# A graph-network kernel: rows of the third pair gathered into unused memory of the sums, six destination loads moved from ScalarE's queue to SyncE's, and x's loads ordered by SyncE's program

## The chip, the core and the metric

The kernel runs on one core of one Trainium2 chip. The metric is the device time in microseconds (us), the median of repeated runs. The engines are named as in the profile: PE (TensorE, with its weight loads as PEld), DVE (VectorE), ACT (ScalarE), POOL (GpSimd) and SP (SyncE, which here only issues transfers). A "q" after an engine's name (SPq, ACTq) marks work of its instruction queue, such as issuing a DMA.

## The reference

One layer of message passing over N = 6250 nodes of 128 features and 100,000 edges, sorted by destination:

```python
msg_in = concat([x[src], x[dst]])            # 100000 x 256
h = relu(msg_in @ Wm1 + bm1)                 # 256 -> 256
h = relu(h @ Wm2 + bm2)                      # 256 -> 256
messages = h @ Wm3 + bm3                     # 256 -> 128
agg = segment_sum(messages, dst) / clip(count(dst), 1)
upd = relu(concat([x, agg]) @ Wn1 + bn1) @ Wn2 + bn2
out = layernorm(x + (x + upd))
```

All inputs are float32, the indices int32.

## The kernel before, in words

The work has three stages.

**Preparation, blocks 0 to 12.** Nodes are taken in 13 blocks of 4 x 128. PE turns a block of x (`turn`, L307) and multiplies it by the two halves of `Wm1` (`products`, L258). The products with the first half, the A table, go through ACT (L266) to device memory (`atab`, stores L267 on SP). The products with the second half, the B table, are split by ACT, DVE and POOL into three bf16 terms, written into seven slots of 768 columns of the third plane of `acc` (`acc[:, HC, ...]`, which is not yet needed for the sums), and stored to `btab` (L276 on SP). The B table runs five blocks behind the A table. ACT, POOL, PE and SP follow the program's order here; DVE is placed by the scheduler. Each load or store on SP also waits, in the built program, until the transfer eight places before it among those of SP and ACT has landed.

x comes in loads of two blocks (`load_x`, L172 on SP). Four of them are held back by a one-column DVE copy that reads the turned block `behind` (L171), so that they are not issued before it. The table `X_LOADS = {0: (4, 6), 1: (6, 8), 3: (8, 10), 5: (10, 12)}` says at the top of which block which load stands. The weights `wu1`, `w3` and `w2` are held back in the same way to block 6 (L189, L191 to L193). In blocks 10 to 12 ACT issues the destinations of the first three pairs of groups (`destinations`, L384: two loads a pair, each broadcast to 64 partitions), held back by a DVE copy from `srcT` (L380).

At the end of preparation PE, ACT and DVE also make the part of the node update that needs x alone (`x_part`, L355, L358, L360), a block at a time, and a small matmul for the bias `b23` (`pb3`, L451, and DVE L452).

**Edges, 98 pairs of groups of 512.** In turn `i` of the loop, `fetch` has POOL gather the A rows of pair `i` with eight indirect DMAs (L492, 128 rows of 1 KB each) and SP load eight windows of B rows (L498; for pair 0 ACT loads four of them). Both go into one of two buffers, `rows`, so the gather of pair `i` waits until the first layer of pair `i - 2` has read its buffer. In the same turn, with `p = i - 1`, the order on PE is: `turned` of pair `p - 3` (L584), `first_layer` of pair `p` (32 transposes L533, then 16 products with a one-hot matrix L540), `sums` of pair `p - 2` (L565), `second_layer` of pair `p - 1` (32 matmuls L555). ACT makes `h1` (L546) and copies the sums (L573); DVE makes the one-hot matrices (`make_hot`, L516, L519), takes the second layer's results (L557) and adds the sums to `acc` (L594).

Before the first sums are added, the seven slots of `acc` are cleared on DVE (`clear`, L644): three in turn `p = 0` ahead of the first layer, two in each of `p = 1` and `p = 2`. One block of `x_part`, number `X_FIRST = 9`, is made in turn `p = 0` behind the first layer, its two results taken by ACT (L358) and DVE (L360).

**Nodes.** The sums are divided, updated, normalised and stored.

## Time and profile before

| | before |
|---|---|
| median of 6 runs | 1707.39 us (1701.44 to 1725.05) |
| the profiled execution | 1709.8 us |
| its span, first to last instruction | 1708.0 us |
| PE busy | 1335.6 us, 78% of the span |
| POOL busy | 811.2 us, 47% |
| granted PE clock over the span | 0.859 of full speed |
| indirect gathers, L492 | 784, 946 ns each at the median |

By stage, from a table of windows of the same execution:

| window, us | what runs | PE busy | granted clock | DMA share |
|---|---|---|---|---|
| 0 to 81.6 | preparation, to pair 0's first transpose | 75.90 | 0.98 | 0.84 |
| 81.6 to 142.8 | pairs 0 to 3 enter the pipeline | 41.06 | 0.81 | 0.42 |
| 142.8 to 1600 | the edge loop | 1119.08 | 0.85 | 0.39 |
| 1600 to 1708 | last pairs and the nodes | 99.59 | 0.97 | 0.32 |

A row of the timeline reads: start and length in us, engine, line of the kernel, operation, what is written from what, how many instructions were merged, and in brackets the idle time before it with what ended that idle time. "issue" means that the engine waited for nothing that the profile shows, "remote" that nothing recorded fits as the releaser. The DMA share is the mean busy share of the core's 16 DMA engines.

### The profile page before, as it was taken

What the parts mean: (1) busy time and instruction counts of PE and PEld (TensorE: products, weight loads), DVE (VectorE), ACT (ScalarE), POOL (GpSimd) and SP (SyncE); (2) the same over time, 40 slices, a digit from 0 to 9 for tenths busy, and PEclk for the clock granted to TensorE, in tenths of its full rate; (3) what the DMA queues carried; (4) which work ended last, traced back from release to release, by engine and by line L of the source; (5) the groups of instructions that cost most, each with busy time, mean ns of one, the idle gap of its engine ahead of it and who ended that gap; (6) DMA issues with size and microseconds to landing.
All of it is one profiled execution on the core that took longest, in us unless ns stands there. A gap on an engine that the chain in (4) does not pass through costs nothing. (4 is left out here: it accounts for less than half of the span.)

```text
span 1708.0 us, 32156 instructions
## 1 busy us (share of the span) xinstructions
PE 1335.6 (78%) x11222; PEld 1054.5 (62%) x11223; DVE 657.0 (38%) x2073; ACT 379.6 (22%) x768; POOL 811.2 (47%) x871
## 2 busy tenths in 40 slices
PE   9868778767777877877877877877788777778898
PEld 8556556656665655656655655665566566666656
DVE  6623323433433333332332332333333333333477
ACT  6412112212221221211211211221122212212136
POOL 8655445445444544445444445544555445445121
PEclk9978888888888888888888888888888888888899
DMA  8744344434434434424434433333443334333143
GB/s 312 260 113 119 94 108 119 114 90 121 114 93 120 117 94 112 114 86 123 113 91 115 108 85 112 106 95 98 112 112 104 92 103 109 93 96 106 40 113 110
DMA packets 167754, 193.69 MB, mean 113 GB/s; under 512 B 31074, under 2 KB 133428, under 8 KB 167572
## 3 DMA queue, kind: packets, MB, share of 16 engines
q0 software_dynamic: 38160, 103.75, 22.5%
q1 hardware_dynamic: 100640, 61.84, 12.3%
q10 hardware_dynamic: 28788, 26.01, 5.4%
q8 instruction: 89, 1.46, 0.4%
q14 instruction: 77, 0.63, 0.1%
HBM read 168.97 MB, written 22.88 MB: 112 GB/s over the span
## 5 line engine op out<-in xcount | busy, mean ns | idle before, releaser
L492 POOL DMA_INDIRECT rows<-atab,srcT x784 | 747.6, 954 | 795.7 <-PE ph L540 560.8
L555 PE MATMUL bank<-w,h 128*128 128x256 f32 x3128 | 710.0, 386 | 0.1
L555 PEld LDWEIGHTS bank<-w,h 128*128 128x128 f32 x3128 | 593.5, 192 | 132.9 <-PE bank L565 54.9
L557 DVE TENSOR_TENSOR h<-bank,nb 128x512 f32<-128x512 f32 x391 | 254.8, 688 | 965.9 <-remote 521.2
L546 ACT ACTIVATE h<-ph,b 128x512 f32<-128x512 f32 x392 | 236.7, 686 | 1239.6 <-PE ph L540 1226.4
L584 PE MATMUL bank<-ident,part 64*128 64x64 f32 x1173 | 103.5, 290 | 335.8 <-DVE h L557 317.3
L584 PEld LDWEIGHTS bank<-ident,part 64*128 64x128 f32 x1173 | 73.6, 184 | 382.6 <-DVE h L557 335.9
L533 PE MATMUL ph<-ident,rows 64*128 64x64 f32 x3128 | 190.3, 299 | 15.4 <-issue 14.2
L533 PEld LDWEIGHTS ph<-ident,rows 64*128 64x128 f32 x3128 | 177.9, 208 | 20.0 <-issue 17.2
L594 DVE TENSOR_TENSOR acc<-acc,bank 128x63 f32 x782 | 171.6, 219 | 33.4 <-DVE acc L594 2.1
L565 PE MATMUL bank<-h,oh 128*32 128x257 f32 x1564 | 150.6, 520 | 0.6 <-ACT part L573 0.6
L540 PE MATMUL ph<-oht,rows 64*128 64x128 bf16 x1564 | 108.6, 300 | 8.4 <-issue 6.4
L540 PEld LDWEIGHTS <-rows 64*128 64x128 bf16 x1564 | 92.9, 142 | 9.3 <-issue 7.2
L516 DVE TENSOR_SCALAR oht<-db,pbase 128x128 bf16<-128x128 int32 x392 | 95.0, 287 | 0.3
L565 PEld LDWEIGHTS bank<-h,oh 128*32 128x32 f32 x1564 | 51.6, 140 | 54.3 <-issue 28.0
L573 ACT COPY part<-bank 128x257 f32<-128x257 f32 x196 | 66.2, 399 | 22.1 <-PE bank L565 14.4
L519 DVE TENSOR_TENSOR oh<-iota_n,dloc 128x128 f32<-128x128 f32 x196 | 55.5, 283 | 0.0
L785 POOL TENSOR_TENSOR agg<-total,rc 128x512 f32<-128x512 f32 (+2 forms) x15 | 16.0, 1076 | 80.0 <-DMA x<-x2tab 41.1
L258 PE MATMUL pbt<-w,xT 128*128 128x256 f32 x196 | 46.4, 383 | 0.2 <-DVE rest L285 0.2
L258 PEld LDWEIGHTS pbt<-w,xT 128*128 128x128 f32 x196 | 36.3, 192 | 6.7 <-issue 1.7
L822 PEld LDWEIGHTS pot<-wu,u 128*128 128x128 f32 x192 | 23.6, 192 | 4.8 <-issue 4.3
L795 PE MATMUL put<-agg,wu 128*128 128x512 f32 (+2 forms) x60 | 23.9, 518 | 0.8 <-POOL agg L785 0.4
(134 smaller groups left out, 420.2 us busy)
## 6 DMA issues: line engine op xcount, KB each, us to landing
rows<-btab SPq DMA_DIRECT2D x778, 32.0 KB
db<-in_dst_dram ACTq DMA_DIRECT2D x194, 128.0 KB
rows<-atab,srcT POOLq DMA_INDIRECT x784
btab<-acc SPq DMA_DIRECT2D x24, 384.0 KB
atab<-at SPq DMA_DIRECT2D x24, 256.0 KB
xd<-in_x_dram SPq DMA_DIRECT2D x12, 256.0 KB
x2tab<-xd SPq DMA_DIRECT2D x12, 256.0 KB
x_sb<-in_x_dram SPq DMA_DIRECT2D x5, 512.0 KB
```

The costliest lines, as they stand in the source:

```text
L258: nc.tensor.matmul(pbt[:, a, :], xT[:, (t0 + a) * P:(t0 + a + 1) * P], w1[:, k, :], start=True, stop=True)
L492: nc.gpsimd.indirect_dma_start(out=ag[:, j, :], out_offset=None, in_=atab[:, :], in_offset=bass.IndirectOffsetOnAxis(ap=idx[:, j:j + 1], a ...
L516: nc.vector.tensor_scalar(ohts[:n, i, k, :], db[:n, k * P:(k + 1) * P], pb_cols[:n, k:k + 1], None, op0=ALU.is_equal)
L533: nc.tensor.matmul(ph[:, i, h, c, u * NQ:(u + 1) * NQ], ag[halves[h], u, c * P:(c + 1) * P], ident[halves[h], halves[h]], is_transpose=Tru ...
L540: nc.tensor.matmul(ph[:, i, h, c, k * P:(k + 1) * P], bw[halves[h], k, c * P:(c + 1) * P], ohts[halves[h], i, k, :], start=False, stop=Tru ...
L546: nc.scalar.activation(h1[:, i, c, :nh * 2 * P].rearrange("p (h e) -> p h e", h=nh), ph[:, i, :nh, c, :], AF.Relu, bias=b1[:, c:c + 1])
L555: nc.tensor.matmul(ph2[:, j - j0, :], h1[:, c, j * P:(j + 1) * P], w2[:, c, :], start=(c == 0), stop=(c == HC - 1))
L557: nc.vector.tensor_tensor(h2[:, j0:j0 + 2, :H], ph2, nb2.to_broadcast([P, 2, H]), op=ALU.max)
L565: nc.tensor.matmul(pg[j * WN:(j + 1) * WN, :H + 1], oh[:, j, :], h2[:, j, :], start=True, stop=True, skip_group_check=True)
L573: nc.scalar.copy(part[:nt * WN, i], pg[:nt * WN, :H + 1])
L584: nc.tensor.matmul(pts[h][:, i, c, :], rows, ident[halves[h], halves[h]], is_transpose=True, start=True, stop=True, skip_group_check=True)
L594: nc.vector.tensor_add(window, window, pts[h][:, i, :, k:k + WB])
```

## The change

Six things are changed together.

1. `fetch` takes the memory for its rows as an argument. For pair 2 (groups 4 and 5) it is `free_rows`, 2560 columns of the third plane of `acc` from slot 3 on. All other pairs keep the two `rows` buffers, which now go to pairs 0, 1, 3, 4, 5 and so on.
2. The slots are cleared in another order: slots 0 to 2 in turn `p = 0` and slots 3 to 6 in turn `p = 2`, both behind the first layer.
3. `x_part(X_FIRST)` is made inside the first layer of pair 0, between the transposes and the one-hot products, with DVE taking both results.
4. The destinations of pairs 0, 1 and 2 are issued by SP in blocks 0, 1 and 2 instead of by ACT in blocks 10, 11 and 12.
5. x's loads stand behind the A stores of their block on SP and lose their DVE copies; `w2` is loaded on SP in block 3 instead of block 6, without a copy.
6. The small matmul for `b23` stands ahead of the third of the last six blocks of `x_part` instead of behind them.

```diff
-            def load_x(b0, b1, behind=None):
+            def load_x(b0, b1):
                 t0, t1 = 4 * b0, 4 * b1
-                if behind is not None:
-                    nc.vector.tensor_copy(x_sb[:, t0, :1], xT[:, behind * 4 * P:behind * 4 * P + 1])
                 nc.sync.dma_start(x_sb[:, t0:t1, :].rearrange("p (b i) d -> p b i d", i=4), xb[:, b0:b1])
...
         def weights(block):
-            for t in (wu1, w3, w2):
+            for t in (wu1, w3):
...
-            nc.sync.dma_start(w2, wm2.rearrange("(k p) h -> p k h", p=P))
...
-        def destinations(g, ng, dst_row):
+        def destinations(g, ng, dst_row, queue=nc.scalar):
             db = ld.tile([P, 2, 2 * P], I32, name="db", bufs=3)
-            if isinstance(g, int) and g < 6:
-                nc.vector.tensor_copy(db[:, 0, :1], srcT[:, 0, :1])
...
-                nc.scalar.dma_start(db[h * NQ:(h + 1) * NQ, :ng, :], edges.to_broadcast([NQ, ng, 2 * P]))
+                queue.dma_start(db[h * NQ:(h + 1) * NQ, :ng, :], edges.to_broadcast([NQ, ng, 2 * P]))
...
         for i in range(BLOCKS):
-            if i in X_LOADS:
-                load_x(*X_LOADS[i], behind=i)
-                if X_LOADS[i][1] == BLOCKS - 1:
-                    nc.sync.dma_start(x_sb[:N - NTF * P, NTF, :], x[NTF * P:, :])
             for n, t0 in enumerate(range(4 * i, min(4 * i + 4, NT), 2)):
...
                 a_table(t0)
+            if i in X_LOADS:
+                load_x(*X_LOADS[i])
+                if X_LOADS[i][1] == BLOCKS - 1:
+                    nc.sync.dma_start(x_sb[:N - NTF * P, NTF, :], x[NTF * P:, :])
+            if i < 3:
+                early.append(destinations(2 * i, 2, dst_row, nc.sync))
+            if i == 3:
+                nc.sync.dma_start(w2, wm2.rearrange("(k p) h -> p k h", p=P))
             b_stores()
...
-            if BLOCKS - 3 <= i:
-                early.append(destinations(2 * len(early), 2, dst_row))
...
         for n, b in enumerate(behind):
+            if n == 2:
+                pb3 = pp.tile([P, 1], F32, name="pb3", tag="pp")
+                for c in range(HC):
+                    nc.tensor.matmul(pb3, w3[:, c, :], b2[:, c:c + 1], start=(c == 0), stop=(c == HC - 1))
+                nc.vector.tensor_add(b23, b3, pb3)
             whole(x_part(b, bank_pb, (nc.vector if n >= len(behind) - 2 else nc.scalar, nc.vector)))
...
-        def fetch(groups, queues):
+        ROWS = (GT + 1) * H
+        FREE = 3
+        free_rows = acc[:, HC, FREE * SLOT:FREE * SLOT + 2 * ROWS].rearrange("p (g r) -> p g r", g=2)
+        assert FREE * SLOT + 2 * ROWS <= SLOTS * SLOT
+        def fetch(groups, queues, rows=None):
-            rows = ld.tile([P, 2, (GT + 1) * H], F32, name="rows", bufs=2)
+            if rows is None:
+                rows = ld.tile([P, 2, ROWS], F32, name="rows", bufs=2)
...
-        def first_layer(got, ohts, nts):
+        def first_layer(got, ohts, nts, between=()):
...
+            whole(between)
...
-        slots = list(range(SLOTS))
+        slots = list(range(SLOTS))[::-1]
...
-                got = fetch([(srcT[:, 2 * i + k, :], firsts[k]) for k in range(2)], [q for q, _ in queues])
+                got = fetch([(srcT[:, 2 * i + k, :], firsts[k]) for k in range(2)], [q for q, _ in queues],
+                            free_rows if i == 2 else None)
...
-            if p == 0:
-                clear(3)
             if p < NP:
                 s = st[p]
-                s["h1"] = first_layer(s.pop("got"), s.pop("ohts"), s["nts"])
-            if p == 0:
-                whole(x_part(X_FIRST, bank, (nc.scalar, nc.vector)))
+                between = x_part(X_FIRST, bank, (nc.vector, nc.vector)) if p == 0 else ()
+                s["h1"] = first_layer(s.pop("got"), s.pop("ohts"), s["nts"], between)
+            if p in (0, 2):
+                clear(FREE if p == 0 else SLOTS - FREE)
...
-            if p in (1, 2):
-                clear(2)
```

More of the change, by code (lines that the diff above doesn't have):

```diff
@@ L447 @@
         for n, b in enumerate(behind):
+            if n == 2:
[3 more added lines that the diff above has]
+                nc.vector.tensor_add(b23, b3, pb3)
             whole(x_part(b, bank_pb, (nc.vector if n >= len(behind) - 2 else nc.scalar, nc.vector)))
-        pb3 = pp.tile([P, 1], F32, name="pb3", tag="pp")
-        for c in range(HC):
-            nc.tensor.matmul(pb3, w3[:, c, :], b2[:, c:c + 1], start=(c == 0), stop=(c == HC - 1))
-        nc.vector.tensor_add(b23, b3, pb3)
     late = ctx.enter_context(tc.tile_pool(name="late", bufs=1))
```

## The prediction

> **What bounds the kernel now.** I read the stages by windows first, then the timelines of POOL and PE over the stretch that the change touches, then the loop behind it.
>
> In preparation PE and the DMA engines are both full:
>
> ```profile
> 8.00:20.00 12.00, 12.00 (x67) 10.60 (x66) 8.32 (x14) 9.20 (x18) 11.63 (x17) 1.00 0.93 325
> 20.00:43.00 23.00, 23.00 (x121) 19.89 (x120) 14.59 (x31) 16.87 (x30) 19.64 (x25) 1.00 0.98 347
> 43.00:56.00 13.00, 12.83 (x57) 9.53 (x56) 9.63 (x13) 8.20 (x16) 11.40 (x14) 1.00 0.97 356
> ```
>
> PE is busy for 12.00 of 12 us, 23.00 of 23 and 12.83 of 13. The last three figures are the granted clock, the DMA share and GB/s. So a transfer moved inside these 48 us finds little room wherever it goes.
>
> Then the pipeline fills. The gathers on POOL, first and last of pairs 0 to 3:
>
> ```profile
> 54.95 1.09 POOL L492 DMA_INDIRECT rows<-atab,srcT  x1 [1.19 <-DMA btab<-acc]
> 74.80 0.95 POOL L492 DMA_INDIRECT rows<-atab,srcT  x1 [0.30 <-issue]
> 86.19 0.94 POOL L492 DMA_INDIRECT rows<-atab,srcT  x1 [10.44 <-DMA rows<-btab]
> 94.97 0.95 POOL L492 DMA_INDIRECT rows<-atab,srcT  x1 [0.30 <-issue]
> 98.67 0.94 POOL L492 DMA_INDIRECT rows<-atab,srcT  x1 [2.75 <-PE ph L540]
> ```
>
> Eight gathers take 9.7 us. Pairs 0 and 1 are done at 75.75, then POOL idles 10.44 us until pair 0's first layer has ended at 85.5. That idle time is what the change aims at. PE over the same stretch:
>
> ```profile
> 78.17 1.98 PE L355 MATMUL pxu<-xT,wu 128*128 128x512 f32 x4 [0.94 <-DVE xT L360]
> 81.64 1.21 PE L533 MATMUL ph<-ident,rows 64*128 64x64 f32 x32 [1.15 <-DVE b L452]
> 85.15 0.34 PE L540 MATMUL ph<-oht,rows 64*128 64x128 bf16 x5 [1.96 <-DMA rows<-btab]
> 85.42 3.63 PE L355 MATMUL bank<-xT,wu 128*128 128x512 f32 x4
> 88.98 1.21 PE L533 MATMUL ph<-ident,rows 64*128 64x64 f32 x32
> 92.11 0.22 PE L540 MATMUL ph<-oht,rows 64*128 64x128 bf16 x1 [1.24 <-issue]
> 98.10 0.29 PE L540 MATMUL ph<-oht,rows 64*128 64x128 bf16 x2 [1.22 <-issue]
> 98.32 9.18 PE L555 MATMUL bank<-w,h 128*128 128x256 f32 x32
> 110.30 0.21 PE L533 MATMUL ph<-ident,rows 64*128 64x64 f32 x1 [1.99 <-issue]
> 112.99 7.17 PE L555 MATMUL bank<-w,h 128*128 128x256 f32 x32
> 125.31 0.90 PE L584 MATMUL bank<-ident,part 64*128 64x64 f32 x11 [4.08 <-DVE h L557]
> ```
>
> The reader should see that PE creeps while a gather runs. From 90.7 to 98.1 the last one-hot products of pair 1 come one at a time, about 1.4 us apart, although nothing they need is missing ("issue"). Pair 2's gather is issued until 95.92, and PE goes on 2.2 us later. Pair 3's gather (to 108.4) stops pair 2's transposes until 111.0, pair 4's (to 122.4) stops the loop until 125.3. Only L555 runs through a gather undisturbed: 32 matmuls in 7.17 us at 112.99. The loop repeats this:
>
> ```profile
> 174.21 1.89 DVE L557 TENSOR_TENSOR h<-bank,nb 128x512 f32<-128x512 f32 x3 [6.80 <-remote]
> 175.55 2.02 PE L533 MATMUL ph<-ident,rows 64*128 64x64 f32 x32
> ```
>
> Pair 7's gather is issued from 162.26 to 172.0; at 174.21 three results of DVE come loose at once, and first layer, next gather, 16.3 us a turn, follow. **A turn is one gather, its 2.2 us tail and some 4.4 us of PE work that the gather does not cover.** A gather is hidden only under L555.
>
> **The change part by part**, as shifts of the end of pair 3's first layer, 128.77 before. Pair 5's gather starts there in both kernels (its buffer is pair 3's), and the loop behind has the same instructions and waits, so a shift there reaches the end unchanged.
>
> *Preparation.* Six destination loads of 128 KB are 786 KB, 2.2 us at 356 GB/s. They leave 43 to 56, where the share is 0.97, and join SP's queue from about 10 us on, where 0.07 x 12 = 0.8 us is free. `w2` (256 KB, 0.7 us) moves up likewise. So at most 0.8 comes out of this, and 2.2 if the freed time comes out whole. Against it stands the load (4, 6): issued near 6.3 before, with its last packet at 10.4, 4.1 us later; now it comes behind block 0's A stores, at about 9.8, would land near 13.9, and its block is turned at 12.96: PE stands 1.0. The load (6, 8), near 12.9, has until 17.29, as long as its 4.1 and 0.3 more; with two or three more transfers ahead of it PE may stand another 2. Behind PE wait ACT's copies, the A stores, and with the last of them the first gather at 54.95. Bounds: 3 lost, 2.2 gained; I take the nearest row's 1.0 lost, since the freed time sits behind a full PE. ACT loses six issues (1.99 + 2.35 + 0.64 + 0.60 = 5.6 us of its queue) and DVE eight copies of 0.15 us; PE is full there and hides both. Uncovered, ACT's waits after them were 1.51, 1.77 and 0.60, all for PE.
>
> The Trainium skill speaks against a transfer gain ("DMA: Bandwidth & Descriptors", Issuing engines are not separate DMA queues): all issuing engines share the same 16 DMA engines, and another issuer saves issue time alone. By that rule nothing is gained on the transfers either, and the term stays at 1.0 lost.
>
> *The gather of pair 2* needs slots 3 to 6, whose last B store has landed when SP starts the B rows at 73.73. It follows pair 1's at 76.05 and ends at 85.8, its tail at 88.0. This takes 9.7 us out of POOL's later queue but lays the gather over the end of `x_part` and pair 0's first layer. ACT's four B-row loads (79.45 to 81.93 before) now fall into the slow stretch. Pair 0's first layer then ends between 85.5 (nothing lost) and 92.5 (the last two loads issued after 88.0 at 0.62 each, 2.48 for four, and 3.2 to land, as from 81.93 to 85.15). I take 90.4: 88.0, four matmuls of `X_FIRST` at 0.43 each, 16 products in 0.65. That is 4.9 late. What queues behind is pair 3's gather, then 90.7 to 100.4.
>
> *X_FIRST* cost 3.63 us at half clock (granted 0.50 from 85.4 to 88.7) between two first layers; inside the wait for B rows it is mostly covered: 3.6 gained, 0 to 3.6 as bounds. Its second result moves from ACT to DVE, 0.75 us, which DVE has free.
>
> *Pair 1's first layer* ran 88.98 to 98.39, 9.4 us, under pair 2's gather. Now it has the 2 to 3 us before pair 3's gather bites (the one at 98.67 left SP's loads quick until 101.8). At 2.9 us, as pair 3's took (125.91 to 128.77), it ends at 93.3; stuck, at 100.4 + 2.2 = 102.6. I take 93.3, since its A rows have long landed.
>
> *Pair 4's gather* then follows pair 3's without a pause, 100.7 to 110.4, tail 112.6. L555 of pair 0 fits below it (93.3 + 9.2 = 102.5, at the slower of its two rates). Pair 2's first layer starts there and sticks, as at 107.44, until 112.6, and ends 1.5 later as then (110.6 to 112.06): 114.1. Pair 5's gather must wait for pair 3, so for once PE runs free: sums 1.07, L555 7.17, L557 and L584 1.6, first layer 2.9, together 12.7: **126.8, or 2.0 earlier**. If pair 1 sticks, the same steps give 115.0 + 1.5 + 12.7 = 129.2, 0.4 later.
>
> *Clearing* stays seven memsets of 0.70 us on DVE. The four in turn 2, 2.8 us, lie under sums and the first bank of L555 (1.07 + 7.17/4 = 2.9); without that cover they would put off L557 by 2.8. The small matmul for `b23` leaves the 1.15 us gap at 81.64, but the last `x_part` results end at 81.5 anyway: 0.1.
>
> **Sum:** 2.0 - 1.0 = 1.0 earlier. The profiled execution (1709.8, its span 1708.0 and 1.8 around it) would become 1708.8; its own time was 2.4 above the median of 1707.39, so the forecast for the median is **1706.4 us**: within 1% (17 us), which is about what a measurement of this kernel can tell from no change.
>
> The Trainium skill ("Runtime: NRT & Kernel Launch", Instruction fetch mechanics) holds that instruction fetch is prefetched and mostly hidden. If so, the creeping would need another cause; by that rule pair 1's first layer costs its 2.9 us under any gather, and the first rival below would be the forecast.
>
> **The rivals.**
>
> *PE slips through the gathers.* For it: at 98 to 107 PE ran L555 undisturbed under a gather. Against it: every turn to 175 shows the stop. Time: PE's own work from 81.64, four first layers (11.6), `X_FIRST` 1.7, two L555 (14.4), the rest 3.7, is 31.4, so 113.0, 15.8 earlier; with 2.2 from preparation 18: 1689. Half way, 1697.
>
> *The gathers crowd the filling, slower.* Pairs 0 to 2, then 3 and 4 leave no pause in which PE gets ahead: L555 of pair 0 creeps too, until 112.6 or 115.0. Then come L555 7.2 to 14.3 (clock 1.00 or 0.50), first layer 2.9, and the 12.7: 137.8 to 144.9, so 9 to 16 later; with 3 lost in preparation 12 to 19: 1719 to 1726. It decides once much less of L555 has run when pair 4's gather starts than the 26 matmuls that 7.4 us (93.3 to 100.7) hold at 0.29 each. For it: the products at 1.4 us each. Against: 7.17 us at 112.99, under a gather.
>
> *The change does not do what it says*, the early gather waiting for pair 0 anyway through the third plane. The stores that it must await are done by 73.73, so I give it little: 1707.
>
> **How the numbers follow.** Forecast 0.48, with the idle rival (0.04) beside it; slipping through 0.26; crowding 0.22. The forecast's own range is 1698 to 1715. Both tails can pass 1%: of the first I put 0.24 beyond (with some for a loop that falls into a quicker beat), of the second 0.20, leaving 0.56 within. The range of 8 in 10 goes from 1687 to 1724.
>
> **What would show it.** POOL's third set of gathers at about 76 with no idle before it; pair 0's first layer ending near 90, pair 1's near 93, pair 3's near 127; one turn without a gather before that; the L533 beat of 16.3 behind it. Pair 3 ending before 115 or after 137 would show a rival right. A changed beat in the loop would make the prediction wrong altogether.

## The result, and the profile after

| | before | changed |
|---|---|---|
| median | 1713.34 us of 80 runs (1695.83 to 1725.14) | 1725.39 us of 38 runs (1705.45 to 1740.17) |
| ratio, over the runs within 1.5% of each kernel's fastest | 1 | 1.0065, interval 1.0047 to 1.0082 |
| the profiled execution, its span | 1709.8, 1708.0 | 1732.2, 1730.5 |
| first gather starts | 54.95 | 61.86 |
| pair 0's first layer ends | 85.49 | 105.61 |
| pair 3's first layer ends | 128.77 | 141.57 |
| last gather starts | 1587.38 | 1609.73 |

The changed kernel is slower by 0.65%, 11 us. The forecast was 1706.4 with a range of 1687 to 1724: no change by its main case, and the measurement lies outside it. Part of the distance is the kernel before's: the six runs that the forecast started from had a median of 1707.39, all 80 have 1713.34. From 1707.39 the measured ratio gives 1718.5, which is inside the range but still 12.1 us above the forecast. The profiled execution of the changed kernel is 6.8 us above its median and that of the kernel before 3.5 below, so these two lie 22.4 us apart. Of this, 12.8 are there when pair 3's first layer ends. The other 9.6 come in the loop behind, whose length differs by more than that between executions of the kernels here (shown below), so the 12.8 is the part to set beside the measured 11.

Where they arise is seen in three places. First PE in preparation: the turn of block 4 before; then, from the changed kernel, SP's issue of the load of blocks 4 and 5, the turn of block 4, the products behind it, and the windows of PE, PEld, DVE, ACT, POOL, clock, DMA share and GB/s.

```profile
12.96 0.60 PE L307 MATMUL pt<-ident,x_sb 128*128 128x128 f32 x4
...
9.43 0.48 SPq L170 DMA_DIRECT2D x_sb<-in_x_dram  x1
...
16.96 1.09 PE L304 MATMUL pt<-ident,x_sb 128*128 128x128 f32 x4 [4.21 <-DMA x_sb<-in_x_dram]
17.84 2.79 PE L255 MATMUL pbt<-w,xT 128*128 128x256 f32 x8
...
8.00:20.00 12.00, 7.79 (x36) 6.52 (x36) 9.53 (x14) 4.93 (x10) 11.96 (x17) 0.86 0.93 280
20.00:48.00 28.00, 28.00 (x148) 24.33 (x148) 12.66 (x23) 20.63 (x37) 18.68 (x24) 1.00 0.99 351
```

PE was busy for 12.00 of the 12 us from 8 to 20, now for 7.79: it stood 4.21 us for the load of blocks 4 and 5, and the eight products behind that ran 2.79 us instead of 1.89, at a granted clock of 0.56 (16.9 to 20). Block 4 is turned at 16.96 instead of 12.96. From 20 on PE is as full as before, so nothing is won back, and the first gather starts 6.9 us later.

Second, POOL, the first gather instruction of pairs 0, 2, 3, 4 and 5:

```profile
61.86 1.09 POOL L494 DMA_INDIRECT rows<-atab,srcT  x1 [1.33 <-issue]
...
82.50 0.95 POOL L494 DMA_INDIRECT acc<-atab,srcT  x1 [0.30 <-issue]
...
105.89 0.95 POOL L494 DMA_INDIRECT rows<-atab,srcT  x1 [13.70 <-PE ph L543]
118.38 0.94 POOL L494 DMA_INDIRECT rows<-atab,srcT  x1 [2.77 <-PE ph L543]
141.85 0.94 POOL L494 DMA_INDIRECT rows<-atab,srcT  x1 [13.77 <-PE ph L543]
```

Pair 2's gather (into `acc`) indeed follows pair 1's without idle time. But the idle time did not go away. It moved behind that gather and grew: 13.70 us until pair 0's first layer ended, where 10.44 stood before. Third, what ACT and PE did meanwhile (L352, L355, L535, L543, L558, L568 and L587 of the changed kernel are L355, L358, L533, L540, L555, L565 and L584 of the kernel before):

```profile
92.27 0.69 ACT L355 ACTIVATE x_sb<-pxu,bu 128x512 f32<-128x512 f32 x1 [16.60 <-remote]
```

```profile
93.00 2.08 PE L352 MATMUL pxu<-xT,wu 128*128 128x512 f32 x2 [13.21 <-ACT x_sb L355]
97.31 3.78 PE L352 MATMUL pxu<-xT,wu 128*128 128x512 f32 x4 [2.23 <-DVE xT L357]
101.93 1.21 PE L535 MATMUL ph<-ident,rows 64*128 64x64 f32 x32 [0.85 <-DVE xT L357]
104.99 0.62 PE L543 MATMUL ph<-oht,rows 64*128 64x128 bf16 x16
108.18 1.84 PE L535 MATMUL ph<-ident,rows 64*128 64x64 f32 x32 [2.57 <-issue]
117.84 0.26 PE L543 MATMUL ph<-oht,rows 64*128 64x128 bf16 x1 [1.90 <-issue]
118.03 9.14 PE L558 MATMUL bank<-w,h 128*128 128x256 f32 x32
132.45 7.17 PE L558 MATMUL bank<-w,h 128*128 128x256 f32 x32
139.97 1.16 PE L535 MATMUL ph<-ident,rows 64*128 64x64 f32 x32
```

From 75.67 to 92.27, while the gathers of pairs 1 and 2 run, ACT does nothing for 16.60 us, and no recorded event releases it. PE waits 13.21 us for that one ACT result in the middle of `x_part`. Pair 0's first layer can only begin at 101.93, before at 81.64. From there on the filling is quicker than it was: 36.0 us from the end of pair 0's first layer to that of pair 3's, against 43.3.

### The profile page after: what moved, and what is told of

The parts are those of the page before. It is cut to its first block, busy times and chain, and to the rows that moved or that the text cites. A ratio compares the mean times of both kernels' runs of the same rounds, so it can differ in the third digit from the quotient of the medians.

```text
span 1730.5 us, 32143 instructions
## 1 busy us (share of the span) xinstructions
PE 1341.3 (78%) x11222; PEld 1056.6 (61%) x11223; DVE 656.5 (38%) x2066; ACT 380.5 (22%) x767; POOL 809.7 (47%) x871
## 5 line engine op out<-in xcount | busy, mean ns | idle before, releaser
L494 POOL DMA_INDIRECT rows<-atab,srcT x776 | 738.9, 952 | 810.1 <-PE ph L543 594.6
L558 PE MATMUL bank<-w,h 128*128 128x256 f32 x3128 | 709.3, 385 | 0.1
L558 PEld LDWEIGHTS bank<-w,h 128*128 128x128 f32 x3128 | 592.7, 192 | 134.8 <-PE bank L568 56.0
L587 PE MATMUL bank<-ident,part 64*128 64x64 f32 x1173 | 104.3, 294 | 330.1 <-DVE h L560 316.4
L587 PEld LDWEIGHTS bank<-ident,part 64*128 64x128 f32 x1173 | 74.6, 187 | 376.4 <-DVE h L560 333.4
L535 PE MATMUL ph<-ident,rows 64*128 64x64 f32 x3096 | 191.0, 301 | 20.3 <-issue 19.4
L535 PEld LDWEIGHTS ph<-ident,rows 64*128 64x128 f32 x3096 | 178.8, 211 | 24.9 <-issue 22.1
L568 PE MATMUL bank<-h,oh 128*32 128x257 f32 x1564 | 153.2, 528 | 0.5 <-ACT part L576 0.5
L543 PE MATMUL ph<-oht,rows 64*128 64x128 bf16 x1548 | 108.0, 301 | 6.0 <-issue 6.0
L543 PEld LDWEIGHTS <-rows 64*128 64x128 bf16 x1548 | 92.2, 142 | 7.2 <-issue 7.2
L568 PEld LDWEIGHTS bank<-h,oh 128*32 128x32 f32 x1564 | 52.0, 142 | 55.5 <-issue 30.9
L352 PE MATMUL pxu<-xT,wu 128*128 128x512 f32 x40 | 21.8, 676 | 16.4 <-ACT x_sb L355 13.2
```

The costliest lines, as they stand in the source:

```text
L494: nc.gpsimd.indirect_dma_start(out=ag[:, j, :], out_offset=None, in_=atab[:, :], in_offset=bass.IndirectOffsetOnAxis(ap=idx[:, j:j + 1], a ...
L535: nc.tensor.matmul(ph[:, i, h, c, u * NQ:(u + 1) * NQ], ag[halves[h], u, c * P:(c + 1) * P], ident[halves[h], halves[h]], is_transpose=Tru ...
L543: nc.tensor.matmul(ph[:, i, h, c, k * P:(k + 1) * P], bw[halves[h], k, c * P:(c + 1) * P], ohts[halves[h], i, k, :], start=False, stop=Tru ...
L558: nc.tensor.matmul(ph2[:, j - j0, :], h1[:, c, j * P:(j + 1) * P], w2[:, c, :], start=(c == 0), stop=(c == HC - 1))
L568: nc.tensor.matmul(pg[j * WN:(j + 1) * WN, :H + 1], oh[:, j, :], h2[:, j, :], start=True, stop=True, skip_group_check=True)
L587: nc.tensor.matmul(pts[h][:, i, c, :], rows, ident[halves[h], halves[h]], is_transpose=True, start=True, stop=True, skip_group_check=True)
```

## The experiments

The runs fell on several chips, and these are of two kinds. On three of them, as in the first comparison, the kernel before takes 1664 to 1713 us; on two it takes 1147.5 and 1147.6. I call the first creeping and the second even, for this is what the traces show. The changed kernel on an even chip (`e15`; the row has busy time, share of the span, instructions):

```profile
PE 1133.4 (98%) x11222; PEld 915.0 (79%) x11223; DVE 681.4 (59%) x2066; ACT 378.9 (33%) x767; POOL 810.0 (70%) x871
```

```profile
101.22 1.22 PE L535 MATMUL ph<-ident,acc 64*128 64x64 f32 x32
```

PE is busy 98% of a span of 1152.6 us. On the chip of the first profile it was 78% of 1730.5. The second line shows pair 2's transposes, all 32 in 1.22 us, between the last instruction of pair 3's gather (to 102.22) and pair 4's gather, which follows at 102.53. POOL's busy time is the same (810.0 against 809.7), and the gathers still take 9.7 us; a loop turn is 10.06 us. So the same instructions under the same gathers creep on one chip and not on another. Each chip was measured in one sitting alone, so whether it is the chip, or a state that it was in at the time, is not told apart. All that the forecast says of creeping holds for the first kind alone.

All runs (the chips are numbered; runs on the same chip were made together, with the same runs of the kernel before):

| run | kernel | chip | median, before | ratio, interval |
|---|---|---|---|---|
| e1 | edges of the change only | even 1 | 1149.6, 1147.5 | 1.0015 (1.0006 to 1.0024) |
| e2 | preparation only | even 1 | 1155.0, 1147.5 | 1.0067 (1.0054 to 1.0080) |
| e3 | changed, pair 2 gathered late | even 1 | 1155.2, 1147.5 | 1.0065 (1.0053 to 1.0078) |
| e4 | changed, plain loads for pair 2 | even 1 | 1158.3, 1147.5 | 1.0098 (1.0084 to 1.0113) |
| e5 | changed | creeping 2 | 1683.3, 1665.3 | 1.0110 (1.0063 to 1.0157) |
| e6 | changed, x ahead | creeping 2 | 1669.5, 1665.3 | 1.0025 (0.9994 to 1.0056) |
| e7 | x ahead, pair 2 late | creeping 3 | 1657.6, 1664.1 | 0.9962 (0.9935 to 0.9989) |
| e8 | x ahead, X_FIRST behind | creeping 3 | 1670.4, 1664.1 | 1.0049 (1.0016 to 1.0083) |
| e9 | x ahead, plain loads for pair 2 | creeping 3 | 1659.9, 1664.1 | 0.9980 (0.9949 to 1.0011) |
| e10 | changed, destinations on ACT | creeping 3 | 1670.0, 1664.1 | 1.0036 (1.0001 to 1.0070) |
| e11 | before | creeping 4 | 1664.0, 1665.5 | 1.0004 (0.9969 to 1.0038) |
| e12 | before, x ahead and destinations on SP | creeping 4 | 1665.8, 1665.5 | 0.9996 (0.9961 to 1.0031) |
| e13 | as e7 | creeping 4 | 1667.0, 1665.5 | 1.0017 (0.9986 to 1.0048) |
| e14 | preparation only | creeping 4 | 1668.5, 1665.5 | 1.0024 (0.9991 to 1.0058) |
| e15 | changed | even 5 | 1153.6, 1147.6 | 1.0047 (1.0034 to 1.0060) |
| e16 | changed, x ahead | even 5 | 1147.2, 1147.6 | 0.9997 (0.9988 to 1.0006) |
| e17 | preparation only | even 5 | 1154.4, 1147.6 | 1.0062 (1.0050 to 1.0074) |
| e18 | x ahead, X_FIRST behind | even 5 | 1146.4, 1147.6 | 0.9989 (0.9978 to 1.0001) |

On creeping chips the intervals are some 0.3% to either side, 5 us. The traces tell why: from the end of pair 3's first layer to the start of the last gather, the same loop took 1397.1 (e7), 1407.2 (e14), 1414.6 (e9), 1416.7 (e11) or 1424.7 us (e12) in single executions. So there I read the filling from the ends of the first layers, and the ratios beside them:

| creeping, us | first gather | pair 0's first layer ends | pair 3's |
|---|---|---|---|
| before: first profile; e11 | 54.95, 54.26 | 85.49, 84.80 | 128.77, 125.18 |
| x ahead, pair 2 late: e12 (X_FIRST behind); e7, e13 (inside) | 55.67; 55.87, 55.16 | 86.08; 89.67, 88.30 | 127.44; 130.53, 128.51 |
| x ahead, plain loads for pair 2: e9 | 54.39 | 88.56 | 126.13 |
| preparation only: e14 | 62.31 | 91.13 | 130.34 |
| x ahead, pair 2 early: e6 (X_FIRST inside); e8 (behind) | 54.28; 54.82 | 97.08; 96.86 | 134.50; 135.07 |
| changed: first profile, e5; with destinations on ACT, e10 | 61.86, 63.20; 60.73 | 105.61, 107.45; 105.65 | 141.57, 145.54; 142.53 |

Single traces scatter here too: the two of the kernel before lie 3.6 us apart at the end of pair 3's first layer, the two of the changed kernel 4.0. The profiled executions of e8 and e10 are 13 and 17 us above their medians; only their first 145 us are used, where e8 agrees with e6 and e10 with the changed kernel.

### e1 to e4: the halves, on an even chip

e1 takes the preparation back (and `w2` to block 6; `b23` stays where the change put it):

```diff
-                load_x(*X_LOADS[i])                  # behind the A stores
+                load_x(*X_LOADS[i], behind=i)        # ahead of them, with its copy
...
-                early.append(destinations(2 * i, 2, dst_row, nc.sync))
...
+                early.append(destinations(2 * len(early), 2, dst_row))   # ACT, blocks 10 to 12
```

> The changed kernel with its preparation put back: x's loads with their copies ahead of the block's A stores, destinations on ACT in blocks 10 to 12, w2 in block 6. The rest of the change stays (pair 2 gathered into the sums' memory, new order of clearing, X_FIRST inside pair 0's first layer). Theory 1 (two losses add, one gain: preparation +7, pair 2's early gather +12, the turn without a gather and X_FIRST -7): first gather back at 55, pair 2's gather near 76, the last x_part results still come only after that gather and its tail, near 88 to 93, pair 0's first layer ends 95 to 99, pair 3's near 134 (5 later than before), ratio to the kernel before 1.003. Theory 2 (the loss is all preparation): pair 0's first layer ends by 90.4 as forecast, pair 3's near 126, ratio 0.998 to 0.999. Theory 3 (the loss is all in the edges): pair 3's first layer ends near 141, ratio 1.0065.

e2 is the kernel before with the same lines the other way round.

> The kernel before with only the preparation of the change: destinations on SP in blocks 0 to 2, x's loads behind the A stores without copies, w2 in block 3. Pair 2 is gathered into its ordinary buffer, clearing and X_FIRST as before. Theory 1: PE stands some 4 us at the turn of block 4, first gather 7 later (62), everything behind it 7 later, pair 3's first layer ends near 136, ratio 1.004. Theory 2 (all preparation): pair 3's first layer near 141, ratio 1.0065. Theory 3 (all edges): PE may stand but the end of x_part hides it, pair 3's first layer within 2 of 128.8, ratio 1.000.

e3 is the changed kernel with pair 2 in its ordinary buffer again, so gathered late:

```diff
-                            free_rows if i == 2 else None)
+                            None)
```

> The changed kernel, only that pair 2 is gathered into the ordinary buffer again, so that its gather waits for pair 0's first layer. Theory 1: x_part is no longer caught by a third gather: pair 0's first layer ends 7 later than before (92), X_FIRST inside it saves 3.6 behind it, pair 3's first layer ends near 132, ratio 1.002. Theory 2 (all preparation): as the changed kernel, 1.0065, or a little less. Theory 3 (all edges, by the early gather): 0.998.

e4 is the changed kernel with plain loads on SP in place of pair 2's indirect transfers:

```diff
+            plain = rows is not None   # pair 2
...
                 for j in range(GT):
+                    if plain:
+                        nc.sync.dma_start(ag[:, j, :], atab[(i * GT + j) * P:(i * GT + j + 1) * P, :])
+                        continue
                     nc.gpsimd.indirect_dma_start(
...
```

> The changed kernel, with the eight indirect transfers of pair 2 replaced by eight plain loads of the same size (128 KB each) from the A table into the same memory, issued by SP: pair 2 then works on rows of other nodes. Theory 1, with the creeping bound to indirect gathers: ACT and PE finish x_part 2 us after pair 1's gather (near 84 plus its tail, 86 to 88), pair 0's first layer ends near 93, pair 3's near 129, ratio 1.000 (0.998 to 1.002). Rival on the cause of the creeping (any megabyte in flight at that place, or the memory of the sums): the last x_part results again come 13 us late, pair 0's first layer ends at 100 or later, ratio 1.004 or more.

All four expectations reckon with engines that creep. On the even chip theory 2 came nearest, and for a reason that it did not name: the preparation costs 7.5 us (0.67%), the edges 2.1 (0.15%), and where nothing creeps an early gather has nothing to hold up. What the 2.1 are I have not traced. Pair 0's first layer ended at 81.26 in e1, although its gathers followed each other from 56.08 to 86.68. e4 missed by far: its eight loads lengthen SP's queue, and pair 4's gather, at 115.20, waited 6.29 us for B rows. It tells nothing of creeping; e9 asks that again.

### e5, e6 and e10: what makes x late

e5 is the changed kernel. e6 moves x's loads on SP:

```diff
         for i in range(BLOCKS):
+            if i in X_LOADS:
+                load_x(*X_LOADS[i])
             for n, t0 in enumerate(...):
                 ...
                 a_table(t0)
-            if i in X_LOADS:
-                load_x(*X_LOADS[i])
```

> The changed kernel itself, beside the kernel before, where the first four experiments ran: there the kernel before took 1147.5 us, PE was busy 99% of the span and the loop repeated every 10.06 us, so nothing crept under the gathers. Theory A (two separate losses, one of preparation, measured at 0.67% by the kernel with the preparation alone, one of the edges, which needs the creeping): if the loop again takes 10.06 us a turn, the preparation's 7 to 8 us stand alone, ratio 1.006 to 1.009, pair 3's first layer ends near 115; if the loop again takes 16.3 us a turn (kernel before near 1713), ratio 1.0065 as in the first comparison, with pair 0's first layer near 105 and pair 3's near 141. Theory B (the loss has nothing to do with preparation): without the creeping, ratio 1.0015 as for the kernel with the edges alone.

> The changed kernel, only that the loads of x stand ahead of the A stores of their block on SP again (without the copies); destinations stay on SP, w2 in block 3, and the edges as changed. Theory A1 (the load of blocks 4 and 5 is late because it stands behind block 0's A stores): it is issued by 6, PE does not stand at the turn of block 4, the first gather starts 5 to 7 earlier than in the changed kernel (near 56), ratio 1.000 to 1.002 at a loop turn of 10.06. Theory A2 (it is late because destinations and w2 crowd the transfers): PE stands all the same, or at a later block, 2 us or more, ratio 1.005 or more. At a turn of 16.3 us: A1 6 us less than the changed kernel, 1.003; A2 1.006.

e10 instead takes the destinations out of SP's queue (`nc.sync` back to ACT in blocks 10 to 12, with the copies) and leaves x behind the A stores.

> The changed kernel with the destinations of the first three pairs issued by ACT in blocks 10 to 12 again, held back by their copies; x's loads stay behind the A stores, w2 in block 3, the edges as changed. Theory A1 (the place behind the A stores alone makes x late): PE stands 3 to 5 us at the turn of block 4, ratio as the changed kernel, 1.0065 to 1.011. Theory A2 (the place and the destination loads together): with 4 us from issue to landing, as the forecast had it, PE stands 1 to 2 us, ratio 1.004 to 1.006.

Block 4's turn in e6 and in e10:

```profile
12.95 0.60 PE L304 MATMUL pt<-ident,x_sb 128*128 128x128 f32 x4
```

```profile
16.53 1.08 PE L304 MATMUL pt<-ident,x_sb 128*128 128x128 f32 x4 [4.12 <-DMA x_sb<-in_x_dram]
```

With x ahead PE turns block 4 at 12.95 without a wait, though destinations and `w2` are still SP's and early. With the destinations gone PE stands 4.12 us, as good as the 4.21 with them. The place behind the A stores is the cause, A1. In e6 SP issues that load before 3.2, in the changed kernel at 9.43. In all nine traces of kernels with that order, on both kinds of chip, PE stood between 3.68 and 4.85 us there. (The copies had a use too: without them the load of blocks 4 and 5 starts at once, beside the one before it, and PE stands 1.43 us for blocks 2 and 3 in e12, 0.78 in e16. In e7 and e13 it stands 1.70 and 1.04 for blocks 6 and 7.) e10's ratio, 1.0036, is lower than A1's 1.0065, but its filling (142.53) is that of the changed kernel; the ratio's interval holds 1.0065.

The Trainium skill ("DMA: Bandwidth & Descriptors", Issuing engines are not separate DMA queues) says that another issuer saves issue time alone. The pair 4.12 and 4.21 does not speak against it, but e10 moves the destinations to other blocks as well, so no run here changes the issuer alone.

On the same chip the changed kernel's ratio (e5) is 0.85% above e6's. On an even chip e15 is 0.50% (5.7 us) above e16, whose ratio is 0.9997, so no loss is left there:

> The changed kernel, now on one chip with its two halves (this call's other runs). Theory A (two losses that add): where engines creep, its ratio less 1 equals the sum of those of the preparation alone and of the early gather with x ahead, 0.5% by the runs so far; pair 3's first layer ends 8 to 10 later than in the kernel before. Theory B (the late preparation and the early gather make each other worse): 0.2% or more over that sum, pair 3's first layer 13 to 20 later, while the two alone stay at 3 to 6 each. Where nothing creeps: the preparation alone, 0.7%.

> The changed kernel with x's loads ahead of the A stores, on the same chip as the changed kernel. Theory A and B: 1.002 to 1.004 where engines creep, pair 0's first layer ends near 97 and pair 3's near 134. Where nothing creeps: 1.000 to 1.0015.

### e7, e9, e12 and e13: the early gather, and what creeping hangs on

e7 is e6 with e3's edit (pair 2 in its ordinary buffer), e9 is e6 with e4's plain loads.

> The changed kernel with x's loads ahead of the A stores again, and pair 2 gathered into the ordinary buffer, so behind pair 0's first layer. Theory A (what the edges lose is the early gather lying over the end of x_part and pair 0's first layer): where the engines creep under gathers, x_part ends near 81, pair 0's first layer near 87, pair 3's between 125 and 129, ratio 0.997 to 1.000. Rival (the edges lose by the rest: X_FIRST inside the first layer, the new order of clearing): pair 3's first layer stays near 134, ratio 1.0025 to 1.004. Where nothing creeps (loop turn of 10.06): within 0.1% of the kernel before by both.

> The changed kernel with x's loads ahead of the A stores again, and the eight indirect transfers of pair 2 replaced by eight plain loads of the same size from the A table into the same memory, issued by SP (pair 2 then works on rows of other nodes). Theory A (only indirect gathers in flight make the engines creep): x_part is free from pair 1's gather end on, its last results come by 82, pair 0's first layer ends by 88, pair 3's near 126 to 129, ratio at most 1.000. Rival (the megabyte itself, or the memory of the sums): the last x_part results come near 91 as with the indirect gather, pair 0's first layer ends near 97, ratio 1.0025 or more. Where nothing creeps: 1.001 to 1.003 by both, as the eight loads lengthen SP's queue.

PE's `x_part` and first transposes in e9, then in e8 (same chip, with the indirect gather of pair 2 from 75.89 on), and ACT in e8:

```profile
76.59 7.44 PE L352 MATMUL pxu<-xT,wu 128*128 128x512 f32 x12 [3.81 <-issue]
84.88 1.21 PE L539 MATMUL ph<-ident,rows 64*128 64x64 f32 x32 [0.84 <-DVE xT L357]
```

```profile
89.87 4.49 PE L352 MATMUL pxu<-xT,wu 128*128 128x512 f32 x6 [9.28 <-ACT x_sb L355]
95.20 1.21 PE L535 MATMUL ph<-ident,rows 64*128 64x64 f32 x32 [0.84 <-DVE xT L357]
```

```profile
89.13 1.27 ACT L355 ACTIVATE x_sb<-pxu,bu 128x512 f32<-128x512 f32 x2 [14.24 <-remote]
```

Without an indirect gather after pair 1's, PE runs 12 matmuls of `x_part` in one piece from 76.59, and the first layer starts at 84.88. With it ACT stops for 14.24 us and the first layer starts at 95.20. In e12 and e13, where no gather follows pair 1's either, the same 12 matmuls run in one piece from 76.47 and 76.66. The second table says the same of every kernel: with pair 2 early, x in time, pair 0's first layer ends at 97, with pair 2 late at 86 to 90; pair 3's 4 to 8 us apart. The times agree: on this chip (creeping 3) e8 has 1.0049, e9 0.9980 and e7 0.9962, and e8's interval overlaps neither of the others. e8 differs from both also in the place of `X_FIRST`, for which the forecast had 0.2%.

The hold need not be one stop of ACT. In e6, the other kernel with pair 2 early and x in time, no wait of ACT in `x_part` is longer than 3.42 us; the steps come late one by one, and PE at last waits for DVE:

```profile
91.86 1.97 PE L535 MATMUL ph<-ident,rows 64*128 64x64 f32 x32 [4.56 <-DVE xT L357]
```

e9 is a weaker test of the cause than it was meant to be. SP issued its plain loads from 87.81 on, behind pair 1's B rows, so they were in flight after the first transposes and not under `x_part`. That `x_part` comes late on these chips when pair 2's indirect gather lies over it is shown; that a plain megabyte there would not do the same is left open.

e7 was faster than the kernel before. e12 (the kernel before with destinations and `w2` moved and x's copies gone, x ahead) and e13 (e7 again) were to say whether that is real and whose it is, with the kernel before (e11) beside them.

> The kernel before itself, for its trace on the chip of the other runs of this call, and for the spread of the comparison: ratio 1.000 within 0.3%. Where engines creep, pair 0's first layer ends near 85.5 and pair 3's between 127 and 131; where they don't, the loop turn is 10.06.

> The kernel before with only these parts of the change: destinations on SP in blocks 0 to 2, w2 in block 3, the copies ahead of x's loads gone (the loads stay ahead of the A stores), b23's matmul earlier. Pair 2's gather, X_FIRST and clearing are those before. Theory A (the gain of the kernel with x ahead and pair 2 late, 0.38%, is the preparation's, freed of copies and of ACT's issues): ratio 0.995 to 0.998, first gather no later than before, ACT's x_part results earlier. Theory B (it is X_FIRST inside pair 0's first layer, and clearing): ratio 0.999 to 1.001.

> The kernel with x's loads ahead of the A stores and pair 2 in the ordinary buffer once more, the best so far (0.9962, interval 0.9935 to 0.9989). Theory A: as the kernel with the preparation's parts alone, within 0.2%, 0.995 to 0.998. Theory B: 0.2 to 0.4% faster than that one. If its gain was chance: 0.999 to 1.001.

It is neither theory's: e13 came out at 1.0017, and its filling was 3.3 us slower than e11's. The 0.9962 may have been the loop's, whose profiled execution is the shortest of all, 1397.1; one execution doesn't show it. No version here is shown to beat the kernel before; the nearest is e18 on an even chip, 0.9989 with an interval up to 1.0001.

### e8 and e18: X_FIRST

Both put `X_FIRST` behind pair 0's first layer again, with x ahead and pair 2 early.

```diff
-            whole(between)
...
-                between = x_part(X_FIRST, bank, (nc.vector, nc.vector)) if p == 0 else ()
-                s["h1"] = first_layer(s.pop("got"), s.pop("ohts"), s["nts"], between)
+                s["h1"] = first_layer(s.pop("got"), s.pop("ohts"), s["nts"])
+            if p == 0:
+                whole(x_part(X_FIRST, bank, (nc.scalar, nc.vector)))
```

> The changed kernel with x's loads ahead of the A stores again, and X_FIRST made behind pair 0's first layer as before (results by ACT and DVE); the early gather stays. The forecast's term (X_FIRST inside the wait for B rows gains 3.6): this kernel is 3 to 4 us slower than the one with x's loads ahead alone, whose ratio was 1.0025, so 1.0045 to 1.005. Rival read from that run's trace (there the one-hot products began at 96.45 as soon as X_FIRST had ended, so the rows were there and no wait was filled): no difference over 1.5 us, ratio 1.002 to 1.0035.

> The changed kernel with x's loads ahead of the A stores and X_FIRST behind pair 0's first layer, on the same chip as the kernel that differs in X_FIRST alone. Reading of the earlier traces: the transposes of pair 1 wait 2.6 us for ACT to have read pair 0's ph when X_FIRST stands inside, and less than 1 us when it stands behind and fills that wait; so the two agree within 1.5 us by this term, pair 0's first to pair 1's first transpose takes 7 to 8 us with X_FIRST inside and 4 to 6 behind. The forecast's term: X_FIRST inside gains 3.6 us, 0.2%.

e8's 1.0049 is what the forecast's term asked for, but e8 and e6 (1.0025) are from different chips, their intervals overlap, and their first layers end within 0.6 us of each other. On one chip e18 is not slower than e16, its median is 0.8 us lower. Pair 1's first transposes in e16 (inside) and e18 (behind):

```profile
84.01 1.21 PE L535 MATMUL ph<-ident,rows 64*128 64x64 f32 x32 [2.56 <-ACT h L549]
```

```profile
81.43 1.21 PE L535 MATMUL ph<-ident,rows 64*128 64x64 f32 x32 [0.65 <-ACT h L548]
```

There is one `ph`, and pair 1 can't enter it until ACT has read pair 0's (four results, 2.42 us). Behind the first layer `X_FIRST` fills that wait; inside, it leaves 2.56 us of it open.

### e14 and e17: the preparation alone, again

> The kernel before with only the changed preparation (destinations on SP in blocks 0 to 2, x's loads behind the A stores without copies, w2 in block 3). Where nothing crept its ratio was 1.0067. Where engines creep: PE stands 4 to 5 us at block 4, first gather 7 to 9 later, everything behind it late by as much, pair 3's first layer near 136 to 138, ratio 1.004 to 1.006 (theory: two losses that add, this one and 3 to 6 us of the early gather). Rival (the early gather's cost covers the late preparation, so that the two don't add): 1.007 to 1.011, all of the changed kernel's loss.

> The kernel before with the changed preparation alone, on the same chip as the changed kernel. Where engines creep: 1.002 to 1.005, first gather at 62, pair 3's first layer ends near 130 to 132 (by the rival that nothing of the late preparation is won back later, 134). Where nothing creeps: 1.0067.

On the even chip e17 repeats e2: 0.62% after 0.67%, 6.8 and 7.5 us that stay. On the creeping chip the first gather is 8.1 us later than e11's, pair 0's first layer 6.3, pair 3's 5.2, and the ratio 1.0024, with an interval that holds 1. The expectation for pair 3 was 136 to 138 and it came out at 130.34: part of the lateness goes into waits that are there anyway. In e14 PE made its 24 matmuls of `x_part` in one piece under pair 1's gather (72.97 to 82.67), and there it was DVE that stood 5.83 us and came late:

```profile
70.64 10.46 PE L352 MATMUL pxu<-xT,wu 128*128 128x512 f32 x24
88.31 1.97 PE L534 MATMUL ph<-ident,rows 64*128 64x64 f32 x32 [6.87 <-DVE b L448]
```

So which engine a gather holds differs from one execution to the next: ACT in the first profile, DVE here. By single traces the two losses add on creeping chips: 5.2 for the preparation (e14 against e11), 7.1 for the early gather and X_FIRST (e6 against e12), 12.3 together, and 12.8 was found in the first profiles. With traces of one kernel 3.6 to 4.0 us apart, so close an agreement is luck. By the ratios they don't show as a sum: on creeping 3 e10, with both losses, has 1.0036, and e8, with x in time, 1.0049. e15 to e18 were meant to settle this on one chip. They fell on an even one, where the whole change (1.0047) costs no more than its preparation alone (1.0062), so whether the two losses add where engines creep stays open.

## Why the prediction was wrong

The forecast's sum for the end of pair 3's first layer, and what the first profile shows:

| step | forecast | measured |
|---|---|---|
| preparation, to the first gather | 1.0 later | 6.9 later |
| pair 0's first layer, beyond that | 4.9 later | 13.2 later (20.1 - 6.9) |
| from its end to pair 3's end | 36.4, 6.9 earlier than 43.3 | 36.0, 7.3 earlier |
| sum | 1.0 earlier | 12.8 later |

**Preparation: mis-sized, 6.9 instead of 1.0.** The step that failed is "at about 9.8, would land near 13.9". SP issued the load at 9.43, as said, but it landed at 16.9, 7.5 us later and not 4.1. The 4.1 was read off the same load in its old place. There it was issued at 6.31, ahead of block 0's two A stores (256 KB each by the list of DMA issues) and of SP's other work, and the DMA engines moved 1.1 MB while it ran (255 GB/s in the window from 6 to 10.4): itself and half a megabyte more. In its new place the two A stores and the index loads that POOL issues from 5.7 on (`dst_i` and `src_i`, 384 KB each) were all under way or in front, and 2.0 MB moved before it had landed (279 GB/s from 9.5 to 13 and 259 from 13 to 17). A duration from issue to landing belongs to a place in the queue, not to the load. That the bytes explain it is read from these rates; no run varies the bytes alone. In e10 256 KB of destinations behind the load are gone and the stand stays, but there the next load of x comes earlier, at 11.26 instead of 12.62. The bound of 3 lost was too narrow too: the stand alone took 4.21, and behind it the turn took 0.5 more and the products 0.9 at the lower clock. Block 12 is turned 5.34 us later than before (48.34 against 43.00). The other 1.6 us to the first gather arise behind it; there POOL's last cast waits 1.39 us for DVE (59.91), where before two casts ran in a row (52.59). Why, I have not traced.

**Pair 0's first layer: mis-sized, 13.2 instead of 4.9, and its bound of 92.5 broken.** The forecast put the early gather over "the end of `x_part` and pair 0's first layer" but let only ACT's loads and the first layer suffer, as if `x_part` finished in time. It had the evidence in hand: in the profile before, ACT's `x_part` results under pair 1's gather already come with idle times of 2.9 to 3.5 us before each:

```profile
70.94 0.69 ACT L358 ACTIVATE x_sb<-pxu,bu 128x512 f32<-128x512 f32 x1 [3.45 <-remote]
74.51 0.69 ACT L358 ACTIVATE x_sb<-pxu,bu 128x512 f32<-128x512 f32 x1 [2.88 <-PE pxu L355]
78.10 0.69 ACT L358 ACTIVATE x_sb<-pxu,bu 128x512 f32<-128x512 f32 x1 [2.90 <-PE pxu L355]
```

`x_part` goes back and forth between PE, ACT and DVE, and one ACT instruction held for 16.60 us stops all of it. The forecast's rule, "A gather is hidden only under L555", was not applied to the stage that the gather was moved onto. It is not exact, since PE's matmuls of `x_part` ran through a gather in e14, but it names the risk that came true here.

**X_FIRST: 3.6 gained became nothing.** In the first profile no wait for B rows is left behind it (the products follow at 104.99). The forecast gave it the wait for B rows as a cover and forgot that it was itself the cover for ACT's reading of `ph`. Pair 1's transposes wait 2.57 us there, and the row of e16 above names ACT's `h1` for such a wait.

**From pair 0 to pair 3: right in its sum, with parts that cancel.** Pair 1 did stick (its first layer ends at 118.10, 12.5 after pair 0's, not 2.9), as the forecast's bound had it. Pair 2's ended 13.4 after that instead of 20.8. The forecast had L555 of pair 0 (9.2) done long before pair 4's gather ended, and then a wait for it. With pair 1 so late, L558 (9.14) lay under that gather almost from its first to its last instruction (118.38 to 128.09), and only the gather's tail was left to wait for (to 130.49). The turn without a gather took 10.06 instead of 12.7.

**Right as told:** pair 2's gather without idle before it, the slots' stores early enough, the turn without a gather, destinations of no account on either queue, the four clears hidden in the turn of 10.06. The loop ran as before: 16.38 us from pair 5's gather to pair 6's.

**The rivals.** The crowding rival's sign was right and its size near (1719 to 1726), but its place wrong, so its number was luck: L555 of pair 0 did not creep, it ran in 9.14; the loss lay ahead of it. Slipping through is what the even chips show, and there it is true of every gather and of the kernel before as well. The forecast used the Trainium skill ("Runtime: NRT & Kernel Launch", Instruction fetch mechanics) as a rule that, if it held, made the creeping go away. That does not follow from the rule alone, since creeping can have another cause. On even chips nothing contradicts that rule. On creeping chips ACT's stop of 16.60 us has no recorded releaser; whether it is instruction fetch no run here shows.

## What to carry over

Ask of a load that is moved past other transfers what is then ahead of it and beside it on all queues, and estimate its time from those bytes; its old time from issue to landing is not its price. Where other engines creep under a long transfer, moving it into idle time of its own queue is a gain only if the others have little to do in that stretch; look for the chain there that hops between engines. And before a piece of work is moved into one wait, look which wait it fills now.

## What the hardware showed beyond that

- The same program took 1147.5 us on some chips and 1664 to 1713 us on others, with the same gathers (9.7 us for eight) and the same POOL time. A turn of the loop is 10.06 us where PE is busy 98%, and 15.2 to 16.0 on average where engines creep (1397.1 to 1468.2 us for 92 turns). A change at this place must be measured on both: e16 has a ratio of 0.9997 on an even chip, and e6, the same kernel, 1.0025 on a creeping one.
- Under two gathers in a row ACT executed nothing for 16.60, 14.24 (e8) or 10.34 and 9.89 us (e5); in e6 it stood no longer than 3.42 us there, and `x_part` was late all the same. The cause is not settled.
- After a stand of 4.21 us PE ran at a granted clock of 0.56 from 16.9 to 20. In the nine traces with such a stand the turn behind it took 1.04 to 1.09 us after 3.75 us or more (eight traces), and 0.63 after 3.68 (e17), where the clock stayed at 1.00.
